# A slot planner in a fused attention kernel that rewards slots holding one value product and nothing else

## The chip, the cores and the metric

The kernel runs on one core of a Trainium2 chip. The metric is the device time of one launch in microseconds (us), the median of three runs. All data is float32.

## What is computed

There are four sequences of 1024 rows with 512 columns. A graph attention block over 20 neighbours comes first (`_L0_cond_ref`), then a transformer block with a modulated layer norm, 16 heads of 64 columns, and an MLP of 2048 columns (`_L1_cond_ref`). The change touches only the attention of the second block:

```python
q, k, v = jnp.split(modulate(layernorm(x), sh_msa, sc_msa) @ W_qkv, 3, axis=-1)   # 16 heads of 64
attn = softmax(einsum('bqhd,bkhd->bhqk', q, k) * 64 ** -0.5, axis=-1)
out  = einsum('bhqk,bkhd->bqhd', attn, v).reshape(B, T, 1024)
x    = x + g_msa * (out @ W_out + b_out)
```

## The kernel before

The order of all instructions on each engine is the order in which the program writes them out. Three stages follow one another: graph attention, attention, and MLP. In the trace of before the attention's first scores start at 420.4 us, and the last slot of the loop starts at 2263.4 us.

**Slots.** The attention is a loop of 256 slots (the loop over `s` in the piece that ends the planner, behind `emit`). There are 64 slots for each of the four sequences (called batches), 8 pairs of heads with 8 blocks of 128 query rows each. Slot s does the softmax of one block for the two heads j = 0 and 1 of a pair:

- `scores` (L1079): TensorE forms 128x1024 scores for both heads, in two PSUM buffers. The next slot writes the same two buffers.
- `largest` (L1090): VectorE takes the maximum over each row, for head 0 and then for head 1.
- `weights` (L1096): ScalarE takes the exponential with the sum of each row. This is the last reader of the scores.
- `scaled` (L1101 to L1105): VectorE takes the reciprocal, then ScalarE scales head 0 (L1103), and GpSimd scales head 1 (L1105).
- `turn` (L1114): VectorE transposes 32x32 blocks, head 0 at the head of the next slot ahead of that slot's maxima, and head 1 after them. At each second slot the transposed weights go out as four DMAs per head on SyncE's queue (`wT<-wd`, L1118).

**Fill.** Beside the scores, each slot issues other work of TensorE. A letter is used for each piece here:

- **A**, a value product (`attend`, L1041): weights times values for two blocks of one pair of heads. It reads wT of two slots, three to five places back. It counts 2 units.
- **P**, an output projection of 128 rows (`project`, L1059), which counts 1 unit. VectorE then adds the PSUM to the residual rows (L1067). In the last of four groups of a batch, VectorE also takes the row statistics (L111, L112), and the rows go out by a DMA on SyncE.
- **Q** and **V**, steps of the chain that forms queries and keys (Q) or values (V) of coming heads (L497). Each unit of work has four steps, the first three of 2 units (V: 2.1), and the last, written **q** or **v** here, of 1. A step leaves copies for ScalarE and, for the second and third step, an addition for VectorE (L511, L515). These wait in the list `later`.
- **T**, transposes of normalised rows for the next batch (`norm_T`, 0.4 units).

`later` is emptied at the head of the next slot, behind `turn` of head 0 and ahead of the maxima. It is emptied in the step's own slot instead, behind that slot's P, if the slot before held no step and the slot has 3 units or more (the last lines of `emit`). Pieces of a slot are issued by their `place`: A is 1, P is 2, T is 3. A chain step is 2.5 if the slot before held a step, and 0.5 otherwise, which puts it ahead of A and P.

**The planner.** Each piece has a first and a last slot (`lo`, `hi` in `fill`). For the chain, `order_chain` searches all orders. For the P, A and T pieces, `order_others` moves one at a time while the cost falls. The two alternate four times. The cost of a slot is `cost_of`: the square of its units, and a penalty if more than two of its pieces need a bank of the pair that A and P share. Loads of weights (`load_qk`, `load_v`) and the sums that GpSimd forms of them (`qk_sums`, `v_sums`, L468 to L471) are tied to chain steps (`behind`) and move with them.

Of the kernel before, what the change touches and what calls it, by code (L numbers as in the profile page):

```python
# [41 lines left out]
def cond_block_kernel(  # L42
# [873 lines left out]
    with ExitStack() as actx:  # L916
# [223 lines left out]
        fill = []  # L1140
# [22 lines left out]
        for b in range(B):  # L1163
            s0 = b * NP * NT
            for kind, n, lo, hi in ORDER:
                first = n < 2 if kind == "qk" else n == 0
                if b == 0 and first:
# [4 lines left out]
                units, load, sums, steps = (  # L1172
                    (1, load_qk, qk_sums, qk_steps) if kind == "qk" else (1.05, load_v, v_sums, v_steps)
                )
# [10 lines left out]
            for gp in range(NP):  # L1185
                g, p = divmod(gp, 2)
                at = s0 + gp * NT
# [61 lines left out]
        for i in range(4):  # L1249
            at = NS - (10, 9, 6, 4)[i]  # L1250
# [19 lines left out]
        where = [f[0] for f in fill]  # L1270
        inside = set(chain)

        def takes(k):

            return fill[k][2], int(k not in inside and fill[k][3] in (1, 2))

        def load_of(ks):
            used = {}
            for k in ks:
                u, n = used.get(where[k], (0, 0))  # L1280
                used[where[k]] = u + takes(k)[0], n + takes(k)[1]
            return used

        def cost_of(u, n):
            return u * u + 4 * max(n - 2, 0) ** 2

        def order_chain():

            used = load_of(k for k in range(len(fill)) if k not in inside)
            values = {where[k] for k, f in enumerate(fill) if f[3] == 1}  # L1290
            first_steps = set(range(0, len(chain), 4))
            best = {(0, 0): (0, ())}
            for s in range(-8, NS):
                new = {}
                for (n, was), (cost, at) in best.items():
                    load, banks = used.get(s, (0, 0))
                    for m in range(2):
                        extra = 0
                        if m > 0:
                            if n == len(chain) or not fill[chain[n]][0] <= s <= fill[chain[n]][1]:  # L1300
                                break
                            load += fill[chain[n]][2]
                            if was and n not in first_steps and s not in values:
                                extra = 3
                        if n + m < len(chain) and fill[chain[n + m]][1] <= s:
                            continue
                        c = cost + cost_of(load, banks) + extra
                        if (n + m, m) not in new or c < new[n + m, m][0]:
                            new[n + m, m] = c, (at, (s,) * m)
                best = new  # L1310
            at = min((best[k] for k in best if k[0] == len(chain)), key=lambda v: v[0])[1]
            slots = []
            while at:
                at, part_ = at
                slots.append(part_)
            for k, s in zip(chain, [s for part_ in reversed(slots) for s in part_]):
                where[k] = s

        def order_others():
            used = load_of(range(len(fill)))  # L1320
            moved = True
            while moved:
                moved = False
                for k, (lo, hi, units, _, _) in enumerate(fill):
                    if k in inside or units == 0:
                        continue
                    u, n = takes(k)

                    def gain(s):

                        a, c = used.get(s, (0, 0))
                        return cost_of(a + u, c + n) - cost_of(a, c)

                    used[where[k]] = used[where[k]][0] - u, used[where[k]][1] - n
                    to = min(range(lo, hi + 1), key=gain)
                    if gain(to) < gain(where[k]) - 1e-9:
                        where[k] = to
                        moved = True
                    used[where[k]] = used.get(where[k], (0, 0))[0] + u, used.get(where[k], (0, 0))[1] + n

        for _ in range(4):
            order_chain()
            order_others()
# [262 lines left out]
```

## Time and profile before

| | us |
|---|---|
| median of three runs (3077.66 to 3081.82) | 3081.66 |
| profiled execution | 3081.5 |
| its span, first to last instruction | 3079.7 |
| busy in the span: TensorE (PE) | 3039.7 |
| VectorE (DVE) | 1984.5 |
| ScalarE (ACT) | 1421.3 |
| GpSimd (POOL) | 1188.8 |
| the slots from the first scores to the start of the last | 1843.0 |

The granted TensorE clock is 0.998 over the span. In the timeline, rows of one kind that follow one another are merged: start, time, engine, line, operation, output and input, and count. A float32 matmul of the program stands as two records, so a slot's four scores are eight rows `psc`, one P is four rows `pout`, one A is 32 rows `pav`, and one Q is eight rows `q`. A slot's length is read from one start of `psc` to the next.

### The profile page before, as it was taken

Reading aid. Unit: us, or ns where it says so; the run is one execution under the profiler, and the core shown is the slowest. Engines: PE = TensorE matmul, PEld = TensorE weight load, DVE = VectorE, ACT = ScalarE, POOL = GpSimd, SP = SyncE. Lnnn points to the kernel's source line nnn. Section 1 sums busy time; section 2 is a strip of 40 time slices with the busy share of each in tenths; the row PEclk is TensorE's granted clock in tenths of the full one; section 3 lists DMA queues with packets and bytes.
Section 4 is the critical chain, followed back from the end, with each engine's and each line's share of the span. In section 5 each row is a group of like instructions: output and inputs, shape, how many; then the busy total and the mean of one; then the engine's idle time right before and its main releaser. Section 6 shows DMA issues by size and latency. Waiting matters only on the chain.

```text
span 3079.7 us, 40763 instructions
## 1 busy us (share of the span) xinstructions
PE 3039.7 (99%) x14977; PEld 1918.1 (62%) x14977; DVE 1984.5 (64%) x2772; ACT 1421.3 (46%) x2351; POOL 1188.8 (39%) x729
## 2 busy tenths in 40 slices
PE   9999999999999999999999999999999999999999
PEld 5666655455455455455455455455468888888888
DVE  3788867777878777878777877777864332223222
ACT  2344446555655555755555755555641221112211
POOL 1444446445454555454654454654531100111010
PEclk9999999999999999999999999999999999999999
DMA  6343438676877776877776877776872011101110
GB/s 193 117 138 106 134 83 200 158 173 156 198 182 177 181 176 158 198 180 176 183 175 157 199 181 175 187 173 150 194 190 88 21 39 37 48 14 42 35 41 14
DMA packets 281882, 418.00 MB, mean 136 GB/s; under 512 B 28272, under 2 KB 100012, under 8 KB 281684
## 3 DMA queue, kind: packets, MB, share of 16 engines
q1 hardware_dynamic: 281436, 415.05, 53.1%
q8 instruction: 120, 1.97, 0.2%
q14 instruction: 78, 0.64, 0.1%
q10 hardware_dynamic: 248, 0.34, 0.0%
HBM read 121.09 MB, written 25.76 MB: 48 GB/s over the span
## 4 chain that ended last, share of the span: by engine, by line
PE 80%; DVE 7%; ACT 4%; issue 3%; POOL 2%; DMA 2%; SPq 2%; POOLq 0%; ACTq 0%; DVEq 0%
PE q L497 17%; PE psc L1079 14%; PE pav L1041 13%; PE pout L1059 6%; PE mbd L497 5%; PE mbu L497 5%; PE mad L497 3%; PE mau L497 3%; ACT w L1096 2%; PE mcd L497 2%; PE mdd L497 2%; PE mdu L497 2%; PE mcu L497 2%; POOL t L733 1%; DVE mx L1090 1%
## 5 line engine op out<-in xcount | busy, mean ns | idle before, releaser
L1105 POOL TENSOR_SCALAR w<-w,sm 128x1024 f32<-128x1024 f32 x256 | 733.9, 2867 | 874.7 <-DVE sm L1101 874.5
L1096 ACT ACTIVATE w<-psc,mx 128x1024 f32<-128x1024 f32 x512 | 570.6, 1114 | 643.0 <-DVE mx L1090 642.5
L1114 DVE STREAM_TRANSPOSE wd<-w 128x1024 f32<-128x1024 f32 x512 | 633.5, 1238 | 126.1 <-ACT w L1103 111.0
L1090 DVE TENSOR_REDUCE mx<-psc 128x1 f32<-128x1024 f32 x512 | 599.6, 1211 | 119.7 <-PE psc L1079 117.6
L1079 PE MATMUL psc<-kT,qT 64*128 64x512 f32 x2048 | 535.8, 617 | 7.8 <-ACT w L1096 5.0
L1041 PE MATMUL pav<-wT,v 128*64 128x256 f32 x4096 | 475.7, 382 | 1.5 <-DMA wT<-wd 1.4
L1041 PEld LDWEIGHTS pav<-wT,v 128*64 128x64 f32 x4096 | 289.0, 137 | 226.2 <-issue 64.8
L1079 PEld LDWEIGHTS psc<-kT,qT 64*128 64x128 f32 x2048 | 203.5, 186 | 264.3 <-issue 145.3
L1103 ACT ACTIVATE w<-w,sm 128x1024 f32<-128x1024 f32 x256 | 291.0, 1137 | 0.0
L1059 PE MATMUL pout<-wout,oT 128*128 128x512 f32 x512 | 245.6, 609 | 0.0
L476 POOL TENSOR_TENSOR tx<-hT 128x512 f32<-128x512 f32 x8 | 10.2, 1271 | 601.1 <-DVE hT L414 601.1
L497 PE MATMUL q<-hT,wqk 128*128 128x512 f32 (+1 forms) x396 | 182.6, 585 | 4.4 <-DVE q L511 4.4
L1059 PEld LDWEIGHTS pout<-wout,oT 128*128 128x128 f32 x512 | 90.2, 189 | 134.0 <-issue 119.2
L710 PE MATMUL pa<-kp,sfT 128*128 128x320 f32 x512 | 143.5, 433 | 1.4 <-ACT sfT L685 1.4
L519 ACT COPY mbu<-mau 128x512 f32<-128x512 f32 x30 | 17.1, 570 | 276.4 <-PE mau L497 276.4
L1067 DVE TENSOR_TENSOR xr<-pout,xr 128x512 f32<-128x512 f32 x128 | 85.5, 678 | 79.6 <-PE pout L1059 79.5
L497 PEld LDWEIGHTS q<-hT,wqk 128*128 128x128 f32 x396 | 73.5, 190 | 100.7 <-issue 87.3
L497 PE MATMUL q<-tx,ex 128*128 128x512 f32 (+1 forms) x264 | 125.0, 597 | 1.0 <-POOL tx L476 1.0
L710 PEld LDWEIGHTS pa<-kp,sfT 128*128 128x128 f32 x512 | 94.8, 190 | 38.2 <-ACT sfT L685 1.9
L670 PE MATMUL pf<-wx,xT 128*128 128x512 f32 x256 | 116.5, 598 | 0.9 <-DVE pf L659 0.9
L497 PE MATMUL mad<-w,hs 128*128 128x256 f32 x512 | 113.1, 379 | 0.0
L497 PEld LDWEIGHTS mad<-w,hs 128*128 128x128 f32 x512 | 97.3, 190 | 13.2
(285 smaller groups left out, 4221.9 us busy)
## 6 DMA issues: line engine op xcount, KB each, us to landing
wT<-wd SPq DMA_DIRECT2D x1024, 256.0 KB
wqk<-in_w_qkv SPq DMA_DIRECT2D x64, 256.0 KB
xT<-in_xt SPq DMA_DIRECT2D x32, 256.0 KB
xs<-in_x SPq DMA_DIRECT2D x32, 256.0 KB
x1d<-xs SPq DMA_DIRECT2D x32, 256.0 KB
xl<-x1d SPq DMA_DIRECT2D x32, 256.0 KB
wv<-in_w_qkv SPq DMA_DIRECT2D x32, 256.0 KB
xr<-x1d SPq DMA_DIRECT2D x32, 256.0 KB
```

The lines of the kernel that those rows point to most:

```text
L497: nc.tensor.matmul(t[:, q * width : (q + 1) * width], lhsT=lhs(which, q, k), rhs=rhs(which, q, k), start=(fresh and q == 0 and k == 0), st ...
L670: nc.tensor.matmul(pfs[i], lhsT=xT[i][:, c, :], rhs=wx[:, c, :], start=False, stop=(c == FC - 1), skip_group_check=True,)
L710: nc.tensor.matmul(pas[i][:, n, :HF], lhsT=sfT2[i][:, c, :], rhs=kp[:, b, c, n * HF : (n + 1) * HF], start=False, stop=(c == FC - 1), skip ...
L1041: nc.tensor.matmul(po[j * D : (j + 1) * D, :], lhsT=vt[b, g][:, m, p * P + j * D : p * P + (j + 1) * D], rhs=w[:, j, :, m, :], start=(m == 0),
L1059: nc.tensor.matmul(po, lhsT=oT[b, 2 * g + p][:, n * P : (n + 1) * P], rhs=wout[b, g][:, p, :], start=(p == 0), stop=(p == 1),)
L1067: nc.vector.tensor_tensor(t, po, t, ALU.add)
L1079: nc.tensor.matmul(sc[j][:, n * F : (n + 1) * F], lhsT=qT[b, gp][q, t * P : (t + 1) * P], rhs=kT[b, gp][q, n * F : (n + 1) * F], start=Tru ...
L1090: nc.vector.tensor_reduce(mx, sc, axis=AX.X, op=ALU.max, negate=True)
L1096: nc.scalar.activation(w, sc, AF.Exp, bias=mx, accum_out=sm)
L1103: nc.scalar.mul(w, w, sm)
L1105: nc.gpsimd.tensor_scalar(w, w, sm, None, ALU.mult)
L1114: nc.vector.transpose(wd[j][:, :, at, :], wn.pop((b, gp, t, j)).rearrange("p (m k) -> p m k", k=U))
```

## The change

`cost_of` gets a third count, the number of value products in a slot. It takes 2 off the cost if a slot holds exactly one value product, no other piece that needs a bank of the pair, and 2 units in all.

```diff
         def takes(k):
 
-            return fill[k][2], int(k not in inside and fill[k][3] in (1, 2))
+            return fill[k][2], int(k not in inside and fill[k][3] in (1, 2)), int(fill[k][3] == 1)
...
-        def cost_of(u, n):
-            return u * u + 4 * max(n - 2, 0) ** 2
+        def cost_of(u, n, v):
+
+            return u * u + 4 * max(n - 2, 0) ** 2 - 2 * (v == 1 and n == 1 and abs(u - 2) < 1e-6)
...
-                        c = cost + cost_of(load, banks) + extra
+                        c = cost + cost_of(load, banks, vals) + extra
...
-                        return cost_of(a + u, c + n) - cost_of(a, c)
+                        at = used.get(s, (0, 0, 0))
+                        return cost_of(*(x + y for x, y in zip(at, it))) - cost_of(*at)
```

The rest of the diff carries the third count along. No piece of work is added or removed. The search comes out with another order. Slots with an A and nothing else of TensorE beside the scores go from 23 to 41 of 256. These slots change (letters in the order of issue, before -> after):

- Batch 0: 16 AP -> A, 17 V -> VP, 19 PQ -> PPQ, 21 PQ -> PPQ, 24 AP -> A, 26 AP -> A.
- Batches 1, 2 and 3 (the numbers of batch 1; add 64 and 128): 72 AQ -> A, 73 PQ -> QP, 74 Aq -> A, 75 PV -> QP, 76 A -> Aq, 80 Av -> A, 81 PQ -> VP, 82 AP -> Av, 83 QP -> PPQ, 84 AP -> AQ, 85 QP -> PPQ. The steps in 77, 78 and 79 keep their letters (V, A, V), but their values are formed one step later. The loads of `load_qk` move from slot 75 to 77, those of `load_v` from 81 to 83, the sums `v_sums` from 73 to 75, and `qk_sums` from 79 to 81.
- All four batches (numbers of batch 0): 30 V -> A, 31 A -> V, 32 VP -> PV.
- Batches 0, 1 and 2 (numbers of batch 0): 48 AP -> A, 49 Q -> QP, 54 AP -> A, 59 Q -> QP.
- The end: 240 PP -> PQ, 241 QA -> A, 242 Q -> QP, 244 AP -> A, 248 AP -> A, 249 Q -> QP, 251 Q -> QP.

Elsewhere the pieces stay where they were, except that some P of equal kind change places with one another.

## The prediction

> **What bounds the kernel now.** I read the page first, then TensorE's timeline slot by slot, then the timelines of VectorE (DVE) and ScalarE (ACT) in those slots, and the waits last.
>
> ```profile
> PE 3039.7 (99%) x14977; PEld 1918.1 (62%) x14977; DVE 1984.5 (64%) x2772; ACT 1421.3 (46%) x2351; POOL 1188.8 (39%) x729
> ```
>
> PE looks full. The Trainium skill (Perfetto Trace Analysis, Identifying the Most-Contended Engine) says that busy share of matmuls is no good measure of the distance to the roofline. The timeline agrees: waits sit inside busy rows. Slot 24, an AP:
>
> ```profile
> 592.31 1.99 PE L1079 MATMUL psc<-kT,qT 64*128 64x512 f32 x8
> 594.23 3.67 PE L1041 MATMUL pav<-wT,v 128*64 128x256 f32 x32
> 597.84 1.98 PE L1059 MATMUL pout<-wout,oT 128*128 128x512 f32 x4
> 599.75 1.99 PE L1079 MATMUL psc<-kT,qT 64*128 64x512 f32 x8
> ```
>
> AP takes 7.44. Slots 88 to 92 are A, QP, A, QP, Aq:
>
> ```profile
> 1059.44 1.99 PE L1079 MATMUL psc<-kT,qT 64*128 64x512 f32 x8
> 1061.36 3.67 PE L1041 MATMUL pav<-wT,v 128*64 128x256 f32 x32
> 1064.96 2.19 PE L1079 MATMUL psc<-kT,qT 64*128 64x512 f32 x8
> ...
> 1072.43 1.99 PE L1079 MATMUL psc<-kT,qT 64*128 64x512 f32 x8
> 1074.35 3.67 PE L1041 MATMUL pav<-wT,v 128*64 128x256 f32 x32
> 1077.95 2.60 PE L1079 MATMUL psc<-kT,qT 64*128 64x512 f32 x8
> ...
> 1085.83 1.99 PE L1079 MATMUL psc<-kT,qT 64*128 64x512 f32 x8
> ```
>
> A alone takes 5.52, 1.92 less than AP. But the scores behind it take 2.19 and 2.60, not 1.99. All 23 A-only slots of before are followed by such a wait of at least 0.19, because of the loop through the softmax. In slot 88 the first maximum starts 2.02 after the slot, the two maxima end at 4.38, and head 1's exponential runs from 4.47 to 5.58. Only then may the next scores of head 1 overwrite its PSUM, 0.13 later. So the wait is (start of first maximum) + 3.56 + 0.13 - (length of the slot). Why 2.60 in slot 91 is seen on DVE in slot 90:
>
> ```profile
> 1072.54 0.69 DVE L1067 TENSOR_TENSOR xr<-pout,xr 128x512 f32<-128x512 f32 x1 [1.23 <-PE pout L1059]
> 1073.14 0.69 DVE L511 TENSOR_TENSOR q<-q,s 128x512 f32<-128x512 f32 x1
> 1073.74 1.24 DVE L1114 STREAM_TRANSPOSE wd<-w 128x1024 f32<-128x1024 f32 x1
> 1074.90 2.31 DVE L1090 TENSOR_REDUCE mx<-psc 128x1 f32<-128x1024 f32 x2
> ```
>
> P ended slot 89, so its addition, the step's addition and the transpose come first, and the maximum starts at 2.47. Behind a short slot, that transpose is late by itself: it waits for L1103, and the maximum starts 2.32 after the end of head 1's exponential.
>
> **The price of a move.** Undelayed lengths from the timeline: A 5.52, AP and Aq 7.44, Q 5.55, V 5.68, PP 5.55, PQ and QP 7.26, PV 7.40, PPQ 8.98, AQ 9.15, Av 7.50, VP 7.41 (PV's row, in the other order). P costs 1.92 behind A, but 1.72 beside a full-array piece. The Trainium skill (TensorEngine Tiling, Key Properties) says that changing the tiling mode drains TensorE, and the rows agree: 0.20 for the switch. By that rule, 18 more A-only slots save 18 x 0.20 = 3.6, and all undelayed lengths together fall by 3.9. By the rows of slots 88 and 89, the wait behind A gives the 0.20 back, so the gain is nil, or a loss where DVE is late. What decides is each stretch with its waits. I carry the two relations above from slot to slot, with the prefix measured.
>
> **Slots 94 to 96 (all four batches): VV A VP -> V A V PV.** Before: 5.98 (second V waits 0.30 for the bank that ACT copies) + 5.52 + 8.24 (0.83 of wait) = 19.74. After: A 5.53, V 5.69 + 0.33 (as slots 14 and 15 show), PV 7.40 + 0.16 = 19.11. Four times -0.63 is **-2.5**. Ends: -0.9 and 0 each.
>
> **Slots 48 to 51 (three batches).** Before 7.61 + 5.55 + 6.77 + 7.43 = 27.36. In slot 50, PE waits 1.05 for the late addition L511. After, slot 49 has 3 units and so empties `later` itself, and that wait goes. The next to come is the maximum in 50 (2.47) and in 51 (3.7, since L515 of 1.05 comes behind a late transpose). A 5.69, QP 7.59, Q 5.55, Aq 8.02: 26.85. Three times -0.51 is **-1.5**. Ends -0.9 and 0.
>
> **Slots 54 to 60 (three batches).** P leaves 54, which is 1.92 shorter. But ACT in slot 56:
>
> ```profile
> 824.78 0.81 ACT L385 ACTIVATE xl<-xl,nm,rs 128x512 f32<-128x512 f32 x1 [1.08 <-DMA xl<-x1d]
> 826.47 0.82 ACT L385 ACTIVATE xl<-xl,nm,rs 128x512 f32<-128x512 f32 x1 [0.87 <-DMA xl<-x1d]
> 827.19 1.09 ACT L1096 ACTIVATE w<-psc,mx 128x1024 f32<-128x1024 f32 x1
> 828.28 1.10 ACT L1096 ACTIVATE w<-psc,mx 128x1024 f32<-128x1024 f32 x1
> ```
>
> The exponentials stand behind rows that wait for a load. Its issue on SP stands behind eight wT issues that follow slot 54's transposes, which P does not move. So slot 57 starts its head 1 at the same time, and the gain in 54 becomes wait in 57. P in 59 is free too: there the next scores wait until 7.42 + 0.13 for the exponential, and QP takes 7.26. Sum **0**. Ends: -1.6 (loads earlier) and +0.3.
>
> **Slots 72 to 86 (batches 1 to 3).** P in 73 and 75 belongs to the last group, so DVE also does statistics (0.69 + 0.18) and SP a store of rows. Placed behind Q, they precede the transpose: slot 74's maximum starts at 3.42, not 2.47. In 75 the wait is 3.42 + 3.53 + 0.13 - 5.52 = 1.56. The row of slots: 5.52, 7.45, 5.52, 8.82, 7.44, 5.70, 5.68, 6.02, 6.48, 7.54, 7.50, 8.98, 9.15, 8.98, 7.44 = 108.22. Slots 72 to 76 are 88 to 92 with the late maximum, 77 to 80 (V A V A) are 13 to 16, and 81 to 86 have slack, so they keep undelayed lengths but for 0.13 in 81. Behind the waiting scores on PE stands the rest of each slot, and DVE's maxima wait for them; behind the statistics on DVE stand transpose and maxima, and ACT's exponentials wait for these. Before, the same slots take 107.90, 107.51 and 107.46. The sum is **+1.8**. The 6.48 of slot 80 contains 0.79 for wT, which slot 16 shows behind the same four pieces; it is 0 to 1.2 (slot 80 of before):
>
> ```profile
> 1001.31 0.65 PE L1041 MATMUL pav<-wT,v 128*64 128x256 f32 x2
> 1002.52 3.64 PE L1041 MATMUL pav<-wT,v 128*64 128x256 f32 x30 [0.56 <-DMA wT<-wd]
> ```
>
> The moved loads (two DMAs of 256 KB each, passing other issues on SP) and sums (four of 0.73 on POOL) keep their distance of two slots from sums to step, some 15 us here; the sums end about 3 us before their step's slot begins. If that cover went, the step would wait for the rest of 2.9. I take 0.
>
> **Slots 16 to 28.** P leaves 24 and 26, and these become exactly 88 to 92: waits 0.20 and 0.62. With 16 to 18 at 21.52 (21.62 before), and two P more in 19 and 21 (3.43), two fewer in 23 to 27 (33.64 for 36.66): **+0.3**.
>
> **The end.** 240 to 246: 50.18 -> 46.51, one P (1.72) less and two stalls less (0.56 in 242, 1.04 in 243). 247 to 254: 53.65 -> 56.42. Slot 249's Q waits for GpSimd (L476), which stands behind that slot's scaling and does not come earlier, so P behind it costs its full 1.7, and P gone from 248 returns nothing. The other P covers waits in 252. Sum **-0.9**, ends -2 and +1.
>
> All: -2.5 - 1.5 + 0 + 1.8 + 0.3 - 0.9 = -2.8. From the profiled execution's own 3081.5 (span 3079.7 and 1.8 around it), 3078.7. The median is 0.16 higher, so **3078.9**.
>
> **Rivals.** *Faster*: the loads in 54 to 57 land earlier, and the 1.6 stays in three batches, -4.8: 3074.1. For it: the slot is shorter and the page's DMA row shows 7 tenths. Against: the issue waits on SP, not on PE. *Slower*: wT becomes the bound in 72 to 82. A needs its weights about 8.4 after the last transpose (slot 16: 7.65 there, 0.78 waited). My margins are 9.1 in 76, 7.6 in 78 and 9.4 in 82. If the loads around them slow the transfers by some 1.5, each of these waits 1.17, as slot 80 did, and 80 itself 0.4 more: 3 x (3 x 1.17 + 0.4) = 11.7, so 3090.6. It decides once the landing takes over 9.5. *As the search counts*: only undelayed lengths matter, -3.9, 3077.8; the wait behind each of 23 A-only slots speaks against it.
>
> **How the numbers follow.** Mine 0.68 (3075 to 3083), faster 0.13, slower 0.12, the search's count 0.07. The range 3073.5 to 3086 leaves out most of the slower rival. A measurement of this kernel tells 0.2% (6.2) from no change. Under 3075.5 lie the faster rival and a tail of mine: 0.18. Over 3087.8 lies the slower rival: 0.12. Within: 0.70.
>
> **What would show it.** Right: `psc` rows over 2.1 behind nearly all 41 A-only slots; about 3.5 for `psc` in slot 75, and 4.7 in 57 with the wait ahead of it; slots 94 to 96 at 19.1; P of 59 without cost. Wrong: `pav` rows over 3.7 with DMA as releaser in 76, 78 and 82; slot 57 no longer than before; sums that make steps wait.

## The result, and the profile after

The changed kernel takes 3084.69 us (median of 22 runs, 3076.36 to 3088.05), and the kernel before, in the same session, 3080.61 (22 runs). The ratio is 1.0012 with a 95% interval of 1.0006 to 1.0017, so by this ratio the change costs 3.7 us (1.8 to 5.2; the two medians stand 4.1 apart), where the forecast was a gain of 2.8. It is within the 0.2% that was forecast as "no change", but on the other side of zero.

The profiled execution has a span of 3082.2 against 3079.7. Its busy row looks like that of before; it says only that PE is busy 2.7 us longer with the same instructions:

```profile
PE 3042.4 (99%) x14977; PEld 1931.8 (63%) x14977; DVE 1983.0 (64%) x2772; ACT 1424.9 (46%) x2351; POOL 1187.7 (39%) x729
```

The timeline says where. I took the start of each slot's first `psc` row and summed the lengths by stretch, for both profiles. All numbers are microseconds, after minus before:

| slots | predicted | found |
|---|---|---|
| 16 to 28 | +0.3 | +0.3 |
| 30 to 32, 94 to 96 and kin (4 times) | -2.5 | -2.0 |
| 48 to 51 and kin (3 times) | -1.5 | -1.2 |
| 54 to 60 and kin (3 times) | 0 | +0.1 |
| 72 to 86 and kin (3 times) | +1.8 | +5.3 |
| 240 to 246 | -3.7 | -3.6 |
| 247 to 254 | +2.8 | +4.6 |
| all slots | -2.8 | +3.4 |

(The last row holds -0.1 from slots that the forecast did not name. The span is 2.5 longer, not 3.4, since the attention starts 0.4 earlier and what follows is 0.5 shorter.) Two rows are off, by 3.5 and by 1.8, and both add wait. Summed over slots 8 to 254, the undelayed lengths of the prediction's list fall by 3.9, as the search counts, but what lies above them (called the stall here) rises from 38.1 to 45.3, by 7.2.

**Slots 72 to 86.** DVE in slot 74 of the changed kernel, to set beside slot 90 of before in the prediction:

```profile
956.28 0.69 DVE L1067 TENSOR_TENSOR xr<-pout,xr 128x512 f32<-128x512 f32 x1 [1.22 <-PE pout L1059]
957.01 0.69 DVE L111 BATCH_NORM_STATS2 st<-xr 128x6 f32<-128x512 f32 x1
957.74 0.18 DVE L112 BATCH_NORM_AGGREGATE mv<-st 128x2 f32<-128x6 f32 x1
957.84 0.68 DVE L511 TENSOR_TENSOR q<-q,s 128x512 f32<-128x512 f32 x1
958.42 1.23 DVE L1114 STREAM_TRANSPOSE wd<-w 128x1024 f32<-128x1024 f32 x1
959.57 2.32 DVE L1090 TENSOR_REDUCE mx<-psc 128x1 f32<-128x1024 f32 x2
```

The slot begins at 956.17. Addition, statistics and the step's addition come ahead of the transpose, and the maxima start at 3.40, close to the 3.42 predicted. On PE this is a `psc` row of 3.17 in slot 75, and then, three slots later, a wait that was not in the row of the forecast:

```profile
962.05 3.17 PE L1079 MATMUL psc<-kT,qT 64*128 64x512 f32 x8 [0.29 <-ACT w L1096]
...
985.90 0.65 PE L1041 MATMUL pav<-wT,v 128*64 128x256 f32 x2
987.30 3.64 PE L1041 MATMUL pav<-wT,v 128*64 128x256 f32 x30 [0.76 <-DMA wT<-wd]
```

The last two rows are slot 78, from 983.95. SyncE's queue shows when that wT was sent:

```profile
974.33 8.79 SPq L1118 DMA_DIRECT2D wT<-wd  x8
983.22 1.06 SPq L945 DMA_DIRECT2D wout<-in_w_out  x1
984.39 1.87 SPq L420 DMA_DIRECT2D wqk<-in_w_qkv  x2
```

Eight issues take 8.8 us one after the other. They begin behind the first late transpose of slot 76 (973.03 to 974.26). PE goes on 4.2 after the end of the last issue, at 987.3.

**Slot 249.** PE in the changed kernel, where slot 249 starts at 2219.97; after that the windows of its wait and of the step (stretch, length, busy time of PE, PEld, DVE, ACT and POOL, then granted clock, DMA share, GB/s):

```profile
2219.97 2.06 PE L1079 MATMUL psc<-kT,qT 64*128 64x512 f32 x8
2224.42 3.64 PE L497 MATMUL q<-tx,ex 128*128 128x256 f32 x8 [2.39 <-POOL tx L476]
2227.85 1.98 PE L497 MATMUL q<-hT,wqk 128*128 128x256 f32 x8
```

```profile
2221.97:2224.37 2.40, 0.06 (x1) 0.00 (x0) 2.40 (x3) 0.91 (x1) 2.40 (x2) 1.00 0.88 211
2224.65:2227.95 3.30, 3.30 (x9) 2.58 (x9) 1.45 (x3) 2.25 (x4) 3.30 (x3) 0.50 0.90 236
```

The same step in the kernel before:

```profile
2226.03 1.99 PE L497 MATMUL q<-tx,ex 128*128 128x256 f32 x8 [0.96 <-POOL tx L476]
```

PE waits 2.39 for GpSimd, where it waited 0.96 before. Then the same eight matmuls take 3.64, where before they took 1.99: the granted clock is 0.50 for 3.4 us. So this wait cost its own length and 1.65 more. The page's busy share, 99% before and after, shows neither.

### The profile page after: what moved, and what is told of

Same layout as the page of the kernel before. It is cut to its first block, busy times and chain, and to the rows that moved or that the text cites. A ratio compares the mean times of both kernels' runs of the same rounds, so it can differ in the third digit from the quotient of the medians.

```text
span 3082.2 us, 40748 instructions
## 1 busy us (share of the span) xinstructions
PE 3042.4 (99%) x14977; PEld 1931.8 (63%) x14977; DVE 1983.0 (64%) x2772; ACT 1424.9 (46%) x2351; POOL 1187.7 (39%) x729
## 4 chain that ended last, share of the span: by engine, by line
PE 84%; DVE 6%; issue 2%; POOL 2%; ACT 2%; SPq 2%; DMA 1%; POOLq 0%; ACTq 0%; DVEq 0%
PE q L497 19%; PE psc L1079 15%; PE pav L1041 14%; PE pout L1059 7%; PE mbd L497 5%; PE mbu L497 5%; PE mad L497 3%; PE mau L497 3%; PE mcd L497 2%; PE mdd L497 2%; PE mdu L497 2%; PE mcu L497 2%; POOL t L733 1%; ACT w L1096 1%; POOL wts L752 1%
## 5 line engine op out<-in xcount | busy, mean ns | idle before, releaser
L1041 PEld LDWEIGHTS pav<-wT,v 128*64 128x64 f32 x4096 | 297.5, 137 | 225.4 <-issue 79.0
L476 POOL TENSOR_TENSOR tx<-hT 128x512 f32<-128x512 f32 x8 | 10.2, 1270 | 601.1 <-DVE hT L414 601.1
```

The lines of the kernel that those rows point to most:

```text
L1041: nc.tensor.matmul(po[j * D : (j + 1) * D, :], lhsT=vt[b, g][:, m, p * P + j * D : p * P + (j + 1) * D], rhs=w[:, j, :, m, :], start=(m == 0),
```

## The experiments

Theory: the loss is local. It sits in 72 to 86, where a P with statistics behind the step delays the transposes and so wT, and in slot 249. Rivals: the new A-only slots cost something each, wherever they lie; loads in flight slow wT; and, on the other side, the softmax loop that the forecast was built on is all that spoils the gain. "Stretch" below is the sum of slots in the profiled run, against before. A ratio is to the kernel before on the same chip.

**The middle as before.** The planner runs without and with the new term (the 2 in `cost_of` becomes `bonus`), and listed slots take the old plan:

```diff
-        for _ in range(4):
-            order_chain()
-            order_others()
...
+        plans = []
+        for bonus in (0, 2):
+            where[:] = [f[0] for f in fill]
+            for _ in range(4):
+                order_chain()
+                order_others()
...
+            plans.append(list(where))
+        keep = ((72, 87), (136, 151), (200, 215))
+        where[:] = [a if any(lo <= a < hi for lo, hi in keep) else c for a, c in zip(*plans)]
```

> Slots 72 to 86 of batches 1 to 3 keep the plan of before, all else is the changed kernel. Local theory (the loss lies in two places, one of them these slots): the three stretches give back the 5.3 us that they cost, so about 5.3 below the changed kernel, 1.9 below before (ratio to before about 0.9994). Rival, an even cost of every new slot with A alone: 9 of 18 such slots go, so half of the whole loss of 3.4 us comes back, 1.7, and the kernel stays about 1.7 to 2 us above before (ratio about 1.0006). In the trace the local theory wants the pav row behind no wait of over 0.3 us in slot 78 and its kin.

Measured: 3080.08 us, ratio 1.0006 (0.9997 to 1.0014). The time is what the even cost wanted, but it does not answer the question. Two P per batch came into 83 and 85 from 87 and 89, whose old slots were not in the list, so 72 to 86 grew by 3.0 to 3.6 and 87 to 92 fell by 2.2 to 2.5. With the slots listed up to 91:

> Slots 72 to 91 of batches 1 to 3 have exactly the plan of before, all else is the changed kernel (in x1_mid_old two projections per batch had been drawn from slots 87 and 89 into 83 and 85, so it was a third plan). Local theory: the three stretches return to the lengths of before, 5.3 us less than in the changed kernel; the kernel 1.9 below before if slot 249 has its half clock, 3.6 below if not (ratio 0.9988 to 0.9994). Even-cost rival: half of the loss stays, about 1.7 above before (ratio 1.0005).

Measured: 3077.57 us, ratio 0.9993 (0.9985 to 1.0002). The stretches stand at -0.3, 0.0 and +0.5, not at +1.4, +1.7 and +2.1. The half clock in slot 249 is there, as in the changed kernel. The ratio is 0.0019 below that of the changed kernel, 5.9 us. So the middle holds more than the whole loss, and an even cost, which wanted 1.0005, lies outside the interval.

**The end as before** (the same edit with `keep = ((239, 300),)`):

> Slots from 239 on keep the plan of before, the rest is the changed kernel. Local theory: slots 240 to 254 together cost the changed kernel 1.0 us (240 to 246 gain 3.6, 247 to 254 lose 4.6), so about 1.0 below the changed kernel and 2.5 above before (ratio about 1.0008), and the window of half TensorE clock in slot 249 (0.53 granted for 3.4 us) is not there. Even-cost rival: 2 or 3 of 18 new slots go, 0.5 back. Both are close in time; the clock window tells them apart: if the wait for GpSimd is not its cause, the window stays near the same time.

Measured: 3081.75 us, ratio 1.0004 (0.9996 to 1.0012). Slots 240 to 254 are back within 0.13 of before, the wait for GpSimd is 1.03, and no half clock follows it there (this profile has another, of 6.8 us, in slot 57). The time is too near both expectations to choose; the clock is not.

**P ahead of the step in slot 249.**

```diff
                     if k in inside:
                         return 2.5 if s - 1 in steps else 0.5
+                    if s in (249,) and fill[k][3] == 2:
+                        return 0.25
                     return fill[k][3]
```

> The changed kernel with one edit: in slot 249 the projection is issued ahead of the first unit of the MLP, not behind it. Local theory: its 1.7 us fill most of the 2.39 us for which TensorE waits for GpSimd (L476), the wait falls to about 0.6, no window of half clock follows (which costs 1.65), and slot 249 falls from 11.50 to about 8.1; the kernel 3.3 us below the changed one, about equal to before (ratio 1.0000). If the half clock has another cause: 1.7 below the changed kernel, window still there. If the idle moves with the piece (GpSimd waits for TensorE in the slot): no change, and the wait stays near 2.4.

Measured: 3079.15 us, ratio 1.0000 (0.9992 to 1.0008). PE in slot 249:

```profile
2222.00 1.98 PE L1059 MATMUL pout<-wout,oT 128*128 128x512 f32 x4
2224.46 1.99 PE L497 MATMUL q<-tx,ex 128*128 128x256 f32 x8 [0.47 <-POOL tx L476]
```

The wait that P now fills falls to 0.47, the step runs at full clock in 1.99, and the slot goes from 11.50 to 8.48. GpSimd does not wait for PE here: its tx comes when it comes. Of the 3.0 gained, 247 to 254 keep 2.75. The time is as forecast, but its interval overlaps that of the changed kernel; it is the profile that shows the repair.

**P ahead of the step in 73, 75 and kin.** The same edit, with the slots 73, 75, 137, 139, 201 and 203.

> The changed kernel with one edit: in slots 73 and 75 and their kin of batches 2 and 3, the projection with the statistics is issued ahead of the chain's step, not behind it. Theory that the statistics ahead of the transpose delay the weights: the first maximum of slots 74 and 76 starts near 2.0 to 2.3 us instead of 3.4 to 3.7, the scores behind 74 no longer wait 1.2, the wait of pav for wT in slot 78 (0.76) goes to under 0.3, and each of the three stretches is 1.5 to 2.5 us shorter: 4.5 to 7.5 below the changed kernel, ratio to before 0.9990 to 0.9997. Rival, the loads in flight (output weights in slot 76, projection weights in 77) slow the transfer of wT: slot 78 still waits 0.5 or more, and only the 1.2 behind slot 74 comes back, 3 to 4 us in all.

Measured: 3076.41 us, ratio 0.9994 (0.9986 to 1.0002). The maxima of slot 74 start at 2.51, not at 3.40 (I had expected 2.0 to 2.3). Slot 75 takes 7.91, not 8.45. The stretches are within 0.05 of before, so 1.5 to 2.1 each came back, 5.2 in all (1.0 of it is lost again in slot 92 and its kin in this profile). On PE, in slots 78, 80 and 249:

```profile
985.24 3.87 PE L1041 MATMUL pav<-wT,v 128*64 128x256 f32 x32
...
998.31 3.03 PE L1041 MATMUL pav<-wT,v 128*64 128x256 f32 x26 [0.72 <-DMA wT<-wd]
...
2219.46 1.99 PE L497 MATMUL q<-tx,ex 128*128 128x256 f32 x8 [2.38 <-POOL tx L476]
```

Slot 78 no longer waits, but slot 80 does now: the wait for wT moved on. Of the 5.2, slots 72 to 77 and their kin, where the late maxima are, give 3.5. Slots 78 to 82 give 1.8: 78 and its kin fall by 3.0 and 81 by 1.5, but 80 rises by 2.2 and 79 by 0.5. And slot 249, which this edit does not touch, has its wait of 2.38 with a step of 1.99. The window of that step:

```profile
2219.47:2222.80 3.33, 3.33 (x15) 2.95 (x16) 1.58 (x4) 2.93 (x6) 3.31 (x3) 1.00 0.90 222
```

The granted clock stays at 1.00. The half clock does not come each time.

**The two loads of 76 and 77 later.**

```diff
-                    behind.append((len(fill), old, 1))
+                    behind.append((len(fill), old, 5 if b > 0 and (kind, n) == ("qk", 4) else 1))
...
-                    add(at + 12, at + 12, 0, 0, load_out, b, g)
-                    add(at + 13, at + 13, 0, 4, gate_out, b, g)
+                    d = 3 if b > 0 and g == 0 else 0
+                    add(at + 12 + d, at + 12 + d, 0, 0, load_out, b, g)
+                    add(at + 13 + d, at + 13 + d, 0, 4, gate_out, b, g)
```

> The changed kernel with two loads of batches 1 to 3 moved: the output weights from slot 76 to 79 and the projection weights from slot 77 to 81 (with the scaling that follows the first). Rival theory, loads in flight slow the transfer of wT: the wait of pav for wT in slots 78, 142 and 206 (slots of 6.8 to 6.9) goes and they come to about 6.1, 2 to 2.5 us in all. Theory of the late transposes: the wT of slot 78 was issued ahead of both loads, so slot 78 still waits 0.5 or more, and only slot 80, whose wT is issued behind them, may gain, at most 0.4 each. Ratio to before 1.0005 by the rival, 1.0010 by the theory.

Measured: 3086.85 us, ratio 1.0027 (1.0016 to 1.0038), a miss for both. Slots 78, 142 and 206 take 6.61, 5.59 and 5.69 (6.92, 6.80, 6.92 in the changed kernel), so in two of three batches the loads did play a part. But slots 80, 144 and 208 rise to 6.95, 6.84 and 6.43 (from 5.87, 6.55, 5.91). And I made a new wait: P in slot 81 waits up to 1.1 for GpSimd's scaling of the output weights (L952), which I had moved too near to it.

**Both repairs, without and with the later loads.**

> The changed kernel with the projection issued ahead of the step in slot 249 and in slots 73 and 75 and their kin. Local theory: the two repairs add up: 6 from the middle stretches (x4_mid_p_first) and 1.7 from slot 249, or 3.4 where its half clock would have come; the kernel 4 to 6 us below before, ratio 0.9980 to 0.9988. If the repairs only move waits (the weights of slot 80, GpSimd later on), it is no better than x4_mid_p_first, 0.9994.

Measured: 3078.12 us, ratio 0.9992 (0.9984 to 1.0001). In the slots the repairs add up: the stretches stand at +0.1, -0.1 and +0.4, and 247 to 254 at +1.9. In time it is no better than the kernel with the middle alone (0.9994), and short of the 0.9980 to 0.9988 expected, though the interval reaches there. Its profile has a new half clock of 6.8 us in slot 185, behind a wait of 1.73 ahead of that slot's first scores, and slot 185 takes 3.4 longer.

> Both repairs (projection ahead of the step in 73, 75 and kin and in 249) with the later loads. With the projection first, slot 78 no longer waits and slot 80 waits for wT (6.7 to 7.0 us instead of 5.5). If the loads in slots 76 and 77, which the synchronization engine issues ahead of that wT, are the cause, slot 80 falls to about 6.0, 2 to 3 us less in three batches than x7_both_p_first; if the 256 KB transfers of wT themselves fill the DMA engines, slot 80 stays at 6.7 or more. Ratio to before 0.9983 by the first, 0.9991 by the second.

Measured: 3081.86 us, ratio 1.0005 (0.9997 to 1.0014). Slots 80, 144 and 208 take 6.81, 7.25 and 7.15. The loads ahead of wT on SyncE are not what makes it late there. The rest above the forecast is the wait in slot 81 again.

**Half of the wT issues from ScalarE.**

```diff
+                eng = nc.scalar if j == 1 and b > 0 and gp == 1 and k in (1, 2) else nc.sync
                 for u in range(4):
-                    nc.sync.dma_start(
+                    eng.dma_start(
```

> The changed kernel with the wT transfers of head 1 that slots 78 and 80 of batches 1 to 3 wait for (four of eight per pair of slots) issued by ScalarE instead of the synchronization engine. The wait of pav for wT went to and fro between 78 and 80 in the runs so far: together they take 12.8 to 13.4 us in the changed kernel and 12.4 to 13.1 with the projection first, where undelayed slots and the 0.3 to 0.5 of late maxima make 11.5. If the eight issues of 1.1 us one after the other are what makes wT late, head 1's weights land up to 4 us earlier, both waits go, and the pair takes about 11.6: 3.5 to 5 us less in three batches, minus up to 0.7 for each exponential that stands behind the four issues. If the bytes are (the 16 DMA engines are 84% busy there), the pair stays at 12.4 or more.

Measured: 3104.49 us, ratio 1.0084 (1.0071 to 1.0098), and no answer. ScalarE in slot 77:

```profile
978.75 6.55 ACTq L1119 DMA_DIRECT2D wT<-wd  x4
985.34 0.37 ACT L1050 COPY oT<-pav 128x256 f32<-128x256 f32 x1 [5.74 <-issue]
985.61 1.03 ACT L1005 COPY kT<-q 128x512 f32<-128x512 f32 x1
```

The four issues hold ScalarE for 6.55 us, and the copy of kT (L1005) that PE needs stands behind them. PE waits 6.1 to 6.8 in slots 77, 141 and 205, with 6.8 us of half clock each time, and so much slack that what 78 and 80 do afterwards says nothing of wT. Whether the eight issues or the bytes set wT (the 16 DMA engines are 84% busy from 960 to 1010 us in the changed kernel) stays open.

**A shorter softmax loop, under both plans.**

```diff
-    nc.vector.tensor_reduce(mx, sc, axis=AX.X, op=ALU.max, negate=True)
+    nc.vector.tensor_reduce(mx, sc[:, : S // 2], axis=AX.X, op=ALU.max, negate=True)
```

> The kernel before, with the maximum of each row taken over the first 512 of its 1024 scores (left out: the second half; the softmax is the same as long as the exponentials stay in range). VectorE's two maxima of 1.2 us become two of about 0.65, so the exponential of head 1 ends some 0.6 earlier in each slot. Loop theory: most of the 13 us of waits behind the 23 slots with A alone go, and some of the late maxima: 6 to 14 us below before. If those waits are not set by the softmax loop, nothing moves.

> The changed kernel with the same shorter maximum (left out: the second half of the scores in it). Loop theory: the undelayed lengths of the changed plan are 3.9 us less in sum, and with the loop shorter the waits behind its 41 slots with A alone no longer give that back; what stays of the loss is the wait for GpSimd in slot 249 (2 to 4 us). So this kernel is 2 below to 1 above its partner with the plan of before, where the pair with the full maximum stands 3.4 to 3.7 apart. Rival, a cost of the new plan that is not the loop (loads, contention, an even cost per slot): it stays 3 us or more above its partner.

Measured: 3053.98 us, ratio 0.9913 (0.9900 to 0.9927), for the plan of before, and 3059.75, ratio 0.9935 (0.9922 to 0.9949), for the changed one. Both fall by about 25 (6 to 14 had been expected of the first), so the loop does set much of the time. But the two plans do not come together, as the loop theory wanted: they stand 5.8 apart, which is the rival's answer. With the loop eased, the stall in the profiles falls from 38.1 to 14.4 in the plan of before, and from 45.3 to only 29.9 in the changed one. (The changed one was profiled in its slowest run, 8.0 above its median, the other 0.9 above. So some 7 of the 15.5 between them belong to that one run.) The waits of PE in the slots (what PE waited for, us in total, times, longest), first with the plan of before, then with the changed one:

```profile
PE pav L1041 <- DMA wT<-wd: 1.2, 2, 0.8
PE q L497 <- POOL tx L476: 0.2, 1, 0.2
```

```profile
PE pav L1041 <- DMA wT<-wd: 5.1, 7, 1.1
PE psc L1079 <- ACT w L1096: 3.6, 3, 1.7
PE q L497 <- POOL tx L476: 2.4, 1, 2.4
```

The middle row is slots 56, 120 and 184, where the exponentials stand behind the rows that wait for `xl` (L385). So the waits that the changed plan has beyond the other are for transfers and for GpSimd. Neither is shorter with the shorter maximum (3.7 and 2.4 in the changed kernel, below).

The same view of the two kernels of this study, before and then after, shows the exchange:

```profile
PE q L497 <- DVE q L511: 4.4, 5, 1.0
PE q L497 <- POOL tx L476: 1.0, 1, 1.0
PE pav L1041 <- DMA wT<-wd: 0.9, 3, 0.6
```

```profile
PE pav L1041 <- DMA wT<-wd: 3.7, 5, 1.2
PE q L497 <- POOL tx L476: 2.4, 1, 2.4
PE q L497 <- DVE q L511: 1.0, 1, 1.0
```

The waits for the addition L511 go, as forecast for slot 50 and its kin; waits for wT and for tx come. But this view holds only gaps between rows, 11.3 us before and 11.6 after over all its lines. The rest of the stall lies inside rows. An undelayed value product takes 3.67; in slot 94 of the changed kernel one takes

```profile
1101.24 4.29 PE L1041 MATMUL pav<-wT,v 128*64 128x256 f32 x32
```

Counted from its first row to its last, gaps included, all value products of slots 8 to 254 together take 6.3 more than 3.67 each in the kernel before, and 14.6 in the changed one. With P first in 73, 75 and kin it is 14.4; with the shorter maximum 7.5 and 16.0. So value products are late by 8.3 more, where the whole stall rises by 7.2, and the late ones are spread more widely than slots 72 to 86. Where a releaser is named, it is mostly wT. Not all of it costs time: 3.8 of the 14.6 lie in slots 56, 120 and 184, where the next scores wait for the exponentials.

**The parts that gained, alone.** The edit of the first experiment with `keep` at 16 to 27, 52 to 60 and kin, and 72 to 91 and kin, and P first in slot 249.

> Only the parts of the change that gained, slot by slot: slots 30 to 32 and kin (-2.0), 48 to 51 and kin (-1.2), and the end with the projection ahead of the step in slot 249 (-3.6 + 1.9); slots 16 to 27, 52 to 60 and 72 to 91 keep the plan of before. If the slot table adds up, 4.9 below before (3075.6 us, ratio 0.9984), and below the changed kernel by 8. If the parts are not independent (a slot's wait decided by what lies far ahead of it), the gain is smaller than 2.

Measured: 3075.01 us, ratio 0.9985 (0.9977 to 0.9993), 4.6 below before. The slots sum to -4.5 where -4.9 was expected. This version beats both kernels, by a little, and the table of stretches adds up for it.

## Why the prediction was wrong

*The price of a move.* Right in its direction. All undelayed lengths fall by 3.9, and `psc` behind A shows the 0.20 (slots 24, 54, 72, 88). But the forecast treated the loop as the one thing that gives it back. The pair with the shorter maximum refutes that: there the changed plan is 5.8 slower though its undelayed lengths are 3.9 less, so waits that a shorter loop does not take away, for transfers and GpSimd, give back more than the whole gain.

*Slots 94 to 96 and 48 to 51.* Both gains came, short by 0.5 and 0.3: -2.0 for -2.5, -1.2 for -1.5. In 48 to 51 the mechanism was right. In 94 to 96 the waits of before went, but the new wait stood in the value product itself (4.03 to 4.31 for 3.67 in slot 94 and its kin), not behind the V. *Slots 16 to 28* and *240 to 246*: right within 0.1.

*Slots 54 to 60.* The sum of 0 held (+0.05, -0.84, +0.86), and so did the reason: slot 54 is 1.92 shorter and slots 56, 120 and 184 grow to 7.64, 6.69 and 8.20. The wait lies ahead of the first scores of 57, so by this count 57 itself is no longer than before (7.51). P in 59 was free: 58 to 60 take 23.48 in both. But one profile can't support such a sum. With this plan in these slots, the same stretch reads -1.1 to +1.5 in profiles without a half clock there, and up to +4.5 with one.

*Slots 72 to 86.* **This step failed**, by 3.5 of the 6.2 between -2.8 and +3.4. Its maxima were right, 3.40 for 3.42, and so was the sum of slots 74 and 75, 14.33 for 14.34. The row then gave slot 78 5.68, hardly more than the undelayed 5.52 of an A: it put the wait for wT there at nothing. Slot 78 and its kin took 6.92, 6.80 and 6.92, with PE waiting for wT. The numbers to see it were in the text: a need of 8.4 after the last transpose, and a margin in 78 of 7.6. I used them as the point at which a rival decides, and did not put the 0.8 into my own row. Measured, PE went on with wT 9.3 after the last transpose (977.96 to 987.30), so it came later than the need of 8.4 too. The 0.3 in slot 77 and the 0.5 and 0.7 in 81 and 209 were missed too; slots 79 and 80 gave some of it back (5.69 and 5.87 for 6.02 and 6.48). The kernel with P first shows how much of it is due to the late transposes: of the 3.5 beyond the forecast, 0.9 lies in slots 72 to 77 and all of that goes, and 2.6 lies in 78 to 82, of which 1.8 goes. (That the stretches end where before stood is partly chance: the maxima that the forecast had counted went as well.) The wait for wT itself moved to slot 80 rather than going, and why wT takes so long stays open.

*The end.* The second step that failed, by 1.8. "P gone from 248 returns nothing" was right: the wait in 249 grew from 0.96 to 2.39. What was not foreseen is the half clock behind it, 1.65, which the forecast put at nothing. In the two profiles where the same wait was followed by full clock, slot 249 took 9.7, below the 10.2 that the forecast's terms make (6.60 before, 1.9 that P in 248 no longer covers, 1.7 for the new P). But 247 to 254 still stand at +3.6 in both, as 254 takes 10.84 and 10.90 (10.19 in the changed kernel). So without the half clock 0.8 more than the forecast remains. In the first of the two PE waits 0.77 for wT in 254; beyond that the cause is open.

*The rivals.* The slower one, wT as the bound, has the mechanism that came, but not its places: 78 and its kin waited, 76 and its kin at most 0.3, 82 not at all, and its 11.7 us did not come there. Over all slots, though, value products do take 8.3 more in sum than before, most often with wT as the named releaser. The faster one did not show. The search's count was refuted by 7.2 us of stall.

*The signs.* `psc` rows over 2.1 stand behind 32 of the 41 A-only slots. In each of the other nine the value product's own rows took 0.36 to 1.40 more than 3.67. `psc` in slot 75 took 3.17, not 3.5, and 3.08 in 57, not 4.7; slots 94 to 96 took 19.30, not 19.1. Of the signs of being wrong, the wait for wT came in 78 and not in 76 or 82.

## What to carry to other kernels

Before a filler is taken out of a slot, list what the next slots wait for that does not depend on the slot's length: a transfer, its row of issues, another engine's queue. The filler's time is returned only down to the first of these. Put your own margins into your own sum: a margin below the need is a wait, not a rival. And a piece that an in-order engine must finish can cost more by what it stands in front of than by its length; here its place within a slot was worth 1.5 to 2.1 us per stretch.

## What the hardware showed that I had not expected

A short wait can cost more than its length. In seven profiles of these kernels PE waited 2.3 to 2.4 us in slot 249. In five of them (the changed kernel, both with the middle as before, the one with the shorter maximum, the one with two queues) the granted clock was then 0.5 for 3.4 us; in two it stayed at 1. In the changed kernel's record the half-clock stretches start at 87.9, 429.2, 2224.6 and 2340.7. From the first, that is 100, 626 and 660 times 3.413 us, so they lie on a fixed grid. Laid over the waits, the grid parts the five from the two. In the five, 2.20 to 2.39 of the wait lie within one window of the grid: in the changed kernel the window is 2221.20 to 2224.61, the wait 2222.03 to 2224.42. In the two an edge splits the wait. With P first in the middle the edge is at 2218.05 and the wait runs from 2217.09 to 2219.46, 0.96 and 1.42 us; with the later loads it is 2.00 and 0.30.

The Trainium skill (TensorE: Matmul & The Clock Gate, What's actually happening) tells of such a free-running window of 3413 ns. It also states that an idle window of about 3.4 us halves the clock. Here 2.20 to 2.39 us of idle time in a window were enough, and the measurement decides. Three profiles also have 6.8 us of half clock right behind waits of 1.30, 1.32 and 1.73 at the head of slots 57, 185 and 185, while a wait of 1.80 at the head of slot 185, in the first kernel with the middle as before, was followed by none. What sets that is open.

This is part of the difference in time as well. The granted clock of the runs averages 0.99800 in the changed kernel (22 runs) and 0.99844 in the kernel before (105 runs, those beside the experiments). An estimate from these is 0.00044 of 3080, or 1.4 us. Each run's clock is recorded to 0.001, which is 3 us by itself, so this is rough. Runs recorded at equal clock differ by 3.1 in the mean (at 0.998) and 2.6 (at 0.999), so most of the 3.7 does not seem to be the clock.
